# Gated layer: one-hots of the slot places on POOL, spread over a whole unit, with the routed blocks in the five units behind it

## Chip, core and metric

The kernel runs on one core of a Trainium2 chip. The metric is the device time of one execution in microseconds (us). The core has five instruction queues that run beside one another and wait for each other through semaphores: PE (matmul; PEld is its weight load), DVE (vector), ACT (activations), POOL (GpSimd, which here also issues the gathers and scatters) and SP (plain DMAs). Each queue works in its own fixed order.

## The reference, cut to what matters

The program is a stack of four layers on an activation of 4 x 512 x 256 in f32; each layer adds an attention-like part and a feed-forward part. The change touches the routed experts of the third layer (index 2) and of the fourth (index 3). In the third layer, seven small experts serve 2048 tokens, two for each token:

```python
logits = x @ router_w + router_b
probs = jax.nn.sigmoid(logits)
scores, idx = jax.lax.top_k(probs, TOPK)          # TOPK = 2, NR = 7 experts
scores = scores / jnp.sum(scores, axis=-1, keepdims=True)
w = jnp.sum(jax.nn.one_hot(idx, NR, dtype=x.dtype) * scores[..., None], axis=-2)
combined = jnp.zeros_like(x)
for e in range(NR):
    combined = combined + w[..., e:e + 1] * expert_ffn(x, r_gate[e], r_up[e], r_down[e])
```

with `expert_ffn(x, g, u, d) = (silu(x @ g) * (x @ u) / 8) @ d`. Beside it, the same layer computes a gated chunk recurrence with 16 heads (q, k, v, s from projections, two scans, a softmax between them, a norm, a gate and an output projection). The fourth layer has a causal attention and eight experts, again two for each token.

## The kernel before, in words

**The routed experts.** A kernel with fixed shapes cannot loop over "the tokens of expert e". So `dispatch` gives every pair (token, choice) a slot: slots are sorted by expert, each expert's share is filled up to whole blocks of 128 slots, and a block has one expert. For the third layer that makes 38 blocks, for the fourth 39. The steps of `dispatch` are: `rank` and `count` by two matmuls, a chain of small DVE operations that ends in `slot`, `v8` and `slots`, then `whole`, `first` and `inside` (block start and place within the block), and then the inversion of the table: which token sits in slot s? It is done by matmul. For each of 16 tiles of 128 tokens and each of the two choices, `place` is a one-hot of 128 x 128 (which of 128 places), `token` is 128 x 38 (the token's number in the column of its block), and `place` times `token` is added up in the PSUM tile `in_slot`. That makes 32 pairs of one-hots and 32 matmuls (64 passes in the trace, since f32 takes two). Both one-hots have four buffers. When the last matmul is done, `in_slot` is copied out as integers, and `experts_of_blocks` finds each block's expert.

**The blocks.** Each routed block passes through four stages: `fetch2` loads the expert's packed weights `we` by SP (the expert's number is read into a register from `expert`) and gathers the 128 rows `r` by an indirect DMA that POOL issues; `features2` finds share and destination (`mine`, `both`, `share`, `to` on DVE) and transposes the rows (`rt` on PE, `rT` on ACT); `hidden2` does the two projections (`gu`), silu on ACT and the product `h` on DVE; `output2` multiplies by the third weight (`o`, L1160), scales it on ACT (`y`) and scatters it to `l_outs` with another indirect DMA on POOL. `r` has three buffers.

**The gated layer.** Its work is cut into 32 units, a pair of heads times a batch entry. A unit is a generator (`gated_unit`), and two others run with it: `gated_supply` prepares the next unit (projections `pj`, exponentials `eF`, their running sum and reciprocals `rz`, transposes) and `gated_drain` finishes the last one (transposes `ot`, output projection `o`, L1382). Inside the unit, `pov` is the second product with the values; behind it DVE computes `o` and `ms`, and POOL computes `rs` and scales `o` with it (L1355 to L1362).

**The order.** `run(u, beside, rate)` takes the 19 steps of a unit in a written order (L1061) and, after each, adds `rate` to a credit; each whole credit takes one step of a second generator `beside`. The credit starts from zero in each unit. In units 0 to 23 `beside` is the other attention of the layer, in units 24 to 29 it is `routed2`, which is `dispatch` followed by the 38 blocks in their four staggered stages. Unit 30 has `ended2` beside it, which collects `l_outs` (`collect`, L364: loads `sum`, additions on POOL and DVE) and starts the fourth layer's norm; unit 31 has `ahead3`. The order that these generators give is a priority; a scheduler then lays the instructions of each queue in order, so the diff alone does not show where they come to lie.

**The fourth layer.** In `layer3` the PE order is the order of the program. `slots_on()` takes a step of that layer's `dispatch` at high priority; steps of two causal attention units stand between the calls. Behind the first call comes `next(units[1])`, which issues the eight `vp` matmuls.

The functions that the diff touches are these:

Of the kernel before, what the change touches and what calls it, by code (L numbers as in the profile page):

```python
# [9 lines left out]
ALU = mybir.AluOpType  # L10
# [32 lines left out]
class Ring:  # L43
# [19 lines left out]
    def tile(self, shape, dtype, tag, name, bufs=None):  # L63
        if self.alias:
            return self.pool.tile(shape, dtype, tag=self.alias, name=name)
        if tag not in self.places and self.pool is None:
            n = 1
            for d in shape[1:]:
                n *= d
            self.places[tag] = [self.base[:, self.free + i * n : self.free + (i + 1) * n] for i in range(bufs)]  # L70
            self.free += bufs * n
            assert self.free <= self.base.shape[1]
        if tag not in self.places:
            return self.pool.tile(shape, dtype, tag=tag, name=name, **({"bufs": bufs} if bufs else {}))
        i = self.turn.get(tag, 0)
        self.turn[tag] = i + 1
        ap = self.places[tag][i % len(self.places[tag])][: shape[0], :]
        if len(shape) == 3:
            ap = ap.rearrange("p (a b) -> p a b", b=shape[2])
        return ap  # L80


class Net:
# [81 lines left out]
    def dispatch(self, moe, rows, top, w, wk, pool, tag, keep=None):  # L165
# [3 lines left out]
        nc = self.nc  # L169
# [43 lines left out]
        slots = tile("slots", P, NTILE, k)  # L213
# [21 lines left out]
        inside, first, less = tile("inside", P, NTILE, k), tile("first", P, NTILE, k), tile("less", P, NTILE)  # L235
# [7 lines left out]
        for i in range(NTILE):  # L243
            for m in range(k):
                place = wk.tile([P, P], F32, tag="place", name="place", bufs=4)
                nc.vector.tensor_scalar(place, self.lane, inside[:, i, m : m + 1], None, ALU.is_equal)
                token = wk.tile([P, blocks], F32, tag="token", name="token", bufs=4)
                nc.vector.tensor_scalar(
                    token, self.starts[:, :blocks], first[:, i, m : m + 1], less[:, i : i + 1], ALU.is_equal, ALU.mult
                )  # L250
                nc.tensor.matmul(
                    ps, place, token, start=(i == m == 0), stop=(i == NTILE - 1 and m == k - 1)
                )
            if i % 2:
                yield
        moe["in_slot"] = in_slot = tile("in_slot", P, blocks, dt=mybir.dt.uint32, of=keep)
        last = nc.vector.tensor_scalar(in_slot, ps, float(NB * T), None, ALU.add)
        with self.tc.issue_after(last.ins):
# [762 lines left out]
    def layer2(self):  # L1021

        nc, a = self.nc, self.a
        UNITS = 8 * NB

        first, beside = 24, 0.44
        moe = self.moe2
        with ExitStack() as ctx:  # L1030
            tp = lambda n, bufs, **k: ctx.enter_context(self.tc.tile_pool(name=n, bufs=bufs, **k))
            self.gp = gp = {"wk": tp("ga", 1), "wk2": tp("ga2", 2), "ps": tp("gaps", 4, space=PSUM)}
            gp["gn"] = gn = gp["wk"].tile([P, 1], F32, tag="gn", name="gn")
            self.load(gn, a["l2_gn"])
            weights, units = self.weights, {}

            def supplied(u):
                pair, b = u // NB, u % NB
                for _ in norms[b]:
                    pass  # L1040
                if pair not in weights:
                    weights[pair] = self.gated_weights(pair)
                units[u] = {"b": b, "w": weights[pair]}
                return self.gated_supply(units[u])

            def normed(b):
                self.layer_norm(b)
                yield
                self.to_features(
                    gp["ps"], self.xn[:, 4 * b : 4 * b + 4, :], self.xnT[:, :, b * T : (b + 1) * T], tag="ps"  # L1050
                )
                yield

            def run(u, beside, rate):


                supply = supplied(u + 1) if u + 1 < UNITS else iter(())
                drain = self.gated_drain(units[u - 1]) if u else iter(())
                credit = 0.0
                chains = {"m": self.gated_unit(units[u]), "s": supply, "d": drain}  # L1060
                for what in "mmmmsmsmmdmmsmsdmsd" if u + 1 < UNITS else "mmmmdmmdmmdmmm":  # L1061
                    next(chains[what], None)
                    credit += rate
                    while credit >= 1:
                        credit -= 1
                        next(beside, None)

            norms = [normed(b) for b in range(NB)]
            for it in (norms[0], supplied(0)):
                for _ in it:  # L1070
                    pass
            with ExitStack() as lctx:
                lp = self.lp
                lp["wk"] = lctx.enter_context(self.tc.tile_pool(name="la", bufs=1))
                lp["w"] = lctx.enter_context(self.tc.tile_pool(name="laps", bufs=4, space=PSUM))
                latent = self.latent_chain()
                for u in range(first):
                    run(u, latent, beside)
                for _ in latent:
                    pass  # L1080
            wk = tp("ex", 4)
            gp["ex"] = tp("exps", 4, space=PSUM)
            self.router3()
            routed = self.routed2(wk)
            for u in range(first, UNITS - 2):
                run(u, routed, 1.45)
            for _ in routed:
                pass
            run(UNITS - 2, self.ended2(wk, gp["ex"]), 0.75)
            run(UNITS - 1, self.ahead3(gp["ex"]), 1.0)  # L1090
            drain = self.gated_drain(units[UNITS - 1])
            for chain in (self.units3[0], self.units3[0], drain, self.units3[0], drain, drain):
                next(chain, None)
        self.held.close()
# [616 lines left out]
    def layer3(self):  # L1711
        nc, a = self.nc, self.a
        with ExitStack() as ctx:
            tp = lambda n, bufs, **k: ctx.enter_context(self.tc.tile_pool(name=n, bufs=bufs, **k))
            self.wexp = tp("wexp3", 4)
            wp = tp("l3w", 1)
            moe = self.moe3
            self.wk3, we = tp("l3k", 2), tp("l3e", 4)
            self.ps3 = ps3 = {n: tp("l3" + n, bufs, space=PSUM) for n, bufs in (("tr", 2), ("sm", 2), ("mm", 4))}
            psm = ps3["sm"]  # L1720


            with self.tc.manual_schedule(engines={mybir.EngineType.PE}):
                units = self.units3
                route = self.route3(NB - 1, psm, "sm")
                with self.tc.high_priority():
                    self.layer_norm3(NB - 1)
                next(units[0])
                for _ in range(2):
                    with self.tc.high_priority():  # L1730
                        next(route)
                    next(units[1])
                next(units[1])
                pieces = self.wexp.tile([P, 3, 4, D], F32, tag="we", name="pieces")
                pieces = Ring(pieces.rearrange("p q e d -> p (q e d)"), None)
                slots = self.dispatch(moe, self.rows, self.top3, self.w3, pieces, psm, "sm", wp)

                def slots_on():
                    with self.tc.high_priority():
                        return next(slots, slots) is None  # L1740

                slots_on()
                next(units[1])
                for n, _ in enumerate(step for pair in zip(units[0], units[1]) for step in pair):
                    if n >= 4:
                        slots_on()
                while slots_on():
                    pass
                for blocks in self.by_blocks(moe, 1):
                    self.blocks3(blocks, we)  # L1750
            self.collect(moe, Ring(self.rows.rearrange("p i d -> p (i d)"), self.small, {"sum": (8, 2, D)}))
# [289 lines left out]
```

## Time and profile before

| what | value |
|---|---|
| median of three runs | 2280.44 us (2271.02, 2280.44, 2280.53) |
| profiled execution, its own time | 2270.34 us |
| its span, first to last instruction | 2268.5 us |
| mean granted PE clock | 0.914 |
| busy: PE, PEld, DVE, ACT, POOL | 1965.4, 1456.1, 1216.4, 834.0, 614.3 us |
| first and last `in_slot` matmul, third layer | 1585.8, 1604.1 us |
| first gather `r` of the third layer | 1605.03 us |
| first and last `in_slot` matmul, fourth layer | 1947.9, 1979.6 us |

All times within an execution count from the start of the span. A timeline row has start, length, queue, line, operation, output and input, shapes and count (x16 is a group of 16 in a row); the bracket at its end is how long the queue stood idle before it, and what released it. PE rows count passes, and an f32 matmul has two. `PEclk` is the share of the full clock that PE was granted.

### The profile page before, as it was taken

The numbers are of one execution on the slowest core, as the hardware profiler recorded it, in microseconds if no ns is written. First come the engines' busy times: TensorE is split into PE (matmuls) and PEld (weight loads), VectorE is DVE, ScalarE is ACT, GpSimd is POOL, SyncE is SP. The second block draws the span as 40 slices with busy tenths as digits, with TensorE's granted clock in tenths as the row PEclk, the third lists the DMA queues.
The fourth block names the chain that finished last, engine by engine and source line by source line (L and its number), as shares of the span: only waits on it lengthen the run. The fifth ranks groups of instructions, "written<-read, shape, count | busy, mean of one in ns | idle before, by whom it ended". The sixth has DMA issues, their size and how long they took to land.

```text
span 2268.5 us, 35445 instructions
## 1 busy us (share of the span) xinstructions
PE 1965.4 (87%) x13143; PEld 1456.1 (64%) x13143; DVE 1216.4 (54%) x3586; ACT 834.0 (37%) x1693; POOL 614.3 (27%) x727
## 2 busy tenths in 40 slices
PE   6754078867999999999999999999899988899995
PEld 2452067754666676666767676666787776678895
DVE  6765056558565555565565655654565664512323
ACT  1110056543334343343344343434254533334321
POOL 5334734343121211211212111111344342022231
PEclk9955599987999999999999999999799989899998
DMA  9921378773000000000000000000443320157696
GB/s 313 325 69 57 115 239 289 252 250 97 1 13 6 6 12 6 8 15 5 3 15 6 6 13 6 24 13 7 139 126 114 106 84 1 55 210 258 208 329 236
DMA packets 145038, 228.89 MB, mean 101 GB/s; under 512 B 15110, under 2 KB 107624, under 8 KB 144712
## 3 DMA queue, kind: packets, MB, share of 16 engines
q1 hardware_dynamic: 130776, 186.82, 25.6%
q0 software_dynamic: 14064, 39.55, 5.0%
q8 instruction: 110, 1.80, 0.3%
q14 instruction: 88, 0.72, 0.1%
HBM read 177.17 MB, written 64.48 MB: 107 GB/s over the span
## 4 chain that ended last, share of the span: by engine, by line
PE 60%; DVE 9%; issue 7%; POOL 5%; DMA 4%; ACT 2%; SPq 0%; POOLq 0%; DVEq 0%; ACTq 0%
PE pt L1269 8%; PE pj L1191 6%; PE o L1382 4%; PE g L1792 4%; PE kq L1607 3%; PE sc L1254 3%; PE pov L1333 3%; PE gu L988 2%; PE qk L1575 2%; DVE junk L1582 2%; DMA r<-l_rows,in_slot 2%; PE o L1805 2%; PE pv L1623 2%; POOL l_outs L360 1%; PE qkp L1883 1%
## 5 line engine op out<-in xcount | busy, mean ns | idle before, releaser
L360 POOL DMA_INDIRECT l_outs<-y,to x156 | 153.4, 983 | 308.9 <-ACT y L359 218.5
L1582 DVE CUSTOM_DVE_ANT_0 junk<-qk,hide 128x512 f32<-128x512 f32 (+3 forms) x256 | 124.5, 486 | 44.2 <-PE qk L1575 25.3
L1792 PEld LDWEIGHTS g<-rT,we 128*128 128x128 f32 x1120 | 132.3, 194 | 6.4 <-ACT rT L353 4.3
L1792 PE MATMUL g<-rT,we 128*128 128x128 f32 x1120 | 133.1, 278 | 3.1 <-ACT rT L353 3.1
L1615 POOL TENSOR_SCALAR_AFFINE_SELECT pr<-pr 128x512 f32<-128x512 f32 x64 | 40.2, 640 | 344.2 <-ACT pr L1612 344.2
L320 POOL DMA_INDIRECT r<-l_rows,in_slot x73 | 71.1, 974 | 220.8 <-PE rt L351 106.8
L1269 PE MATMUL pt<-Wg,xnT 128*128 128x256 f32 x512 | 127.6, 403 | 2.2 <-ACT h L1154 1.0
L1382 PE MATMUL o<-Wo,oT 128*128 128x256 f32 x512 | 124.2, 385 | 0.0
L1269 PE MATMUL pt<-Wv,xnT 128*128 128x256 f32 x512 | 121.1, 388 | 0.0
L1260 DVE TENSOR_TENSOR s<-sc,keep 128x512 f32<-128x512 f32 x128 | 82.3, 682 | 71.2 <-PE sc L1254 71.2
L1269 PEld LDWEIGHTS pt<-Wg,xnT 128*128 128x128 f32 x512 | 99.8, 201 | 27.6 <-issue 6.3
L1204 DVE RECIPROCAL rz<-rz 128x128 f32<-128x128 f32 x128 | 117.2, 933 | 0.4
L439 PE MATMUL tr<-ident,xn 128*128 128x128 f32 x160 | 36.6, 371 | 92.2 <-DVE xn L424 85.1
L988 PE MATMUL gu<-rT,we 128*128 128x128 f32 x664 | 98.3, 287 | 19.9 <-issue 6.9
L359 ACT ACTIVATE y<-o,share 128x256 f32<-128x256 f32 x156 | 74.0, 474 | 110.1 <-PE o L1805 41.1
L332 DVE TENSOR_TENSOR mine<-r,number 128x2 f32<-128x2 f32 (+2 forms) x90 | 14.8, 164 | 185.0 <-DMA r<-l_rows,in_slot 168.9
L988 PEld LDWEIGHTS gu<-rT,we 128*128 128x128 f32 x664 | 90.9, 198 | 30.9 <-issue 16.0
L1269 PEld LDWEIGHTS pt<-Wv,xnT 128*128 128x128 f32 x512 | 95.4, 192 | 15.2 <-issue 0.2
L1612 ACT ACTIVATE pr<-kq 128x512 f32<-128x512 f32 (+1 forms) x192 | 86.2, 530 | 49.5 <-PE kq L1607 49.0
L1382 PEld LDWEIGHTS o<-Wo,oT 128*128 128x128 f32 x512 | 96.5, 198 | 8.2 <-issue 0.5
L353 ACT COPY rT<-rt 128x256 f32<-128x256 f32 x156 | 57.0, 371 | 117.0 <-PE rt L351 95.8
L1607 PE MATMUL kq<-q,kT 32*128 32x128 f32 (+3 forms) x512 | 89.7, 491 | 7.7 <-DVE mx L1582 5.9
(485 smaller groups left out, 4426.0 us busy)
## 6 DMA issues: line engine op xcount, KB each, us to landing
we<-l_packed SPq DMA_DIRECT2D x121, 384.0 KB
we<-l_w SPq DMA_DIRECT2D x70, 512.0 KB
we<-l_wo SPq DMA_DIRECT2D x35, 512.0 KB
l_rows<-none SPq DMA_DIRECT2D x1, 12920.0 KB
r<-l_rows SPq DMA_DIRECT2D x16, 680.0 KB
xn<-l_outs SPq DMA_DIRECT2D x32, 256.0 KB
l_rows<-xn SPq DMA_DIRECT2D x8, 544.0 KB
l_packed<-l_w_gate SPq DMA_DIRECT2D x1, 4096.0 KB
```

The lines of the kernel that those rows point to most:

```text
L359: nc.scalar.activation(y, ps, AF.Copy, scale=share)
L360: self.no_order(moe["name"] + " back", nc.gpsimd.indirect_dma_start(out=moe["outs"][:, :], out_offset=bass.IndirectOffsetOnAxis(ap=to, axi ...
L988: nc.tensor.matmul(ps[:, q, :], we[:, q, k * P : (k + 1) * P], rT[:, k, :], start=(k == 0), stop=(k == KD - 1))
L1191: nc.tensor.matmul(ps, w[n][:, k, :], self.xnT[:, k, t["b"] * T : (t["b"] + 1) * T], start=(k == 0), stop=(k == KD - 1))
L1204: inverse = lambda c: nc.vector.reciprocal(rz[:, c * P : (c + 1) * P], rz[:, c * P : (c + 1) * P])
L1260: nc.vector.tensor_tensor(s, ps[hh], keep4, ALU.mult)
L1269: nc.tensor.matmul(ps[:, i, :], self.xnT[:, k, s : s + P], w[n][:, k, :], start=(k == 0), stop=(k == KD - 1))
L1382: nc.tensor.matmul(ps[:, p, :], of_parity(oT[:, h, c * D : (c + 1) * D], p), wo[:, h, :], start=(h == 0), stop=(h == 1),)
L1582: nc.vector.tensor_tensor_reduce(out=junk[:, :m], in0=tiles[j][:, off : off + m], in1=self.hide[:, T - m :], op0=ALU.add, op1=ALU.max, sca ...
L1607: nc.tensor.matmul(tiles[j][:, BLOCK[i] - off : BLOCK[i] - off + T - i * P], kT[r, i * P : (i + 1) * P], qT[r, i * P :], start=True, stop= ...
L1612: nc.scalar.activation(pr[:, j, off : off + m], tiles[j][:, :m], AF.Exp, scale=0.25)
L1792: nc.tensor.matmul(pt[:, m, :], we[:, q, k * T + m * P : k * T + (m + 1) * P], rT[:, k, :], start=(k == 0), stop=(k == KD - 1),)
```

## The change

There are three edits. In `dispatch`, `place` is made by POOL (`nc.gpsimd`) where the experts are those of the third layer, and by DVE elsewhere; and the loop over the 16 tiles yields after each tile, where it yielded after every second. In `layer2`, the first of the six units takes 0.95 steps of `routed2` for each of its own and the other five take 1.62, where all took 1.45. In `layer3`, `slots_on` takes two steps of `dispatch` at each call where it took one, at its first call too.

```diff
@@ dispatch
         for i in range(NTILE):
             for m in range(k):
                 place = wk.tile([P, P], F32, tag="place", name="place", bufs=4)
-                nc.vector.tensor_scalar(place, self.lane, inside[:, i, m : m + 1], None, ALU.is_equal)
+                (nc.gpsimd if moe is self.moe2 else nc.vector).tensor_scalar(place, self.lane, inside[:, i, m : m + 1], None, ALU.is_equal)
                 token = wk.tile([P, blocks], F32, tag="token", name="token", bufs=4)
...
-            if i % 2:
-                yield
+            yield
         moe["in_slot"] = in_slot = tile("in_slot", P, blocks, dt=mybir.dt.uint32, of=keep)
@@ layer2
             for u in range(first, UNITS - 2):
-                run(u, routed, 1.45)
+                run(u, routed, 0.95 if u == first else 1.62)
             for _ in routed:
                 pass
@@ layer3
                 def slots_on():
                     with self.tc.high_priority():
-                        return next(slots, slots) is None
+                        return next(slots, slots) is None and next(slots, slots) is None
```

## The prediction

> **What bounds the kernel now.** I read the page's shares and slices first, then the PE timeline around the routed work of the gated layer, the stretches with their granted clock, the DVE and POOL timelines of the same stretch, the groups by shape for POOL's prices, and last the PE timeline at the start of layer 3, because the diff touches `slots_on` there.
>
> ```profile
> PE 1965.4 (87%) x13143; PEld 1456.1 (64%) x13143; DVE 1216.4 (54%) x3586; ACT 834.0 (37%) x1693; POOL 614.3 (27%) x727
> PEclk9955599987999999999999999999799989899998
> ```
>
> PE is the bound: 87% busy. In the clock row, slice 28 (1588 to 1645 us) shows 7 where the gated layer otherwise has 9. That is where the one-hots of the slot places lie.
>
> ```profile
> core 0: us, PE busy (x) PEld busy (x) DVE busy (x) ACT busy (x) POOL busy (x), PEclk, DMA share, GB/s
> 1585.00:1588.00 3.00, 2.90 (x23) 2.37 (x24) 2.97 (x16) 0.00 (x0) 0.00 (x0) 0.94 0.37 123
> 1588.00:1609.00 21.00, 19.81 (x86) 18.97 (x86) 15.90 (x67) 0.59 (x1) 3.00 (x3) 0.50 0.32 103
> 1609.00:1612.00 3.00, 3.00 (x22) 2.55 (x21) 1.70 (x12) 0.87 (x3) 0.73 (x1) 0.57 0.98 319
> ```
>
> From 1588 to 1609 us PE is nominally full, but at clock 0.50, and POOL is nearly idle. The `in_slot` matmuls (38 columns) keep PE occupied without keeping its clock up.
>
> ```profile
> 1594.64 9.87 PE L251 MATMUL in_slot<-token,place 128*128 128x38 f32 x46
> 1605.70 3.33 PE L1333 MATMUL pov<-v,s 128*128 128x128 f32 x14 [1.19 <-DVE of L276]
> 1617.05 0.70 PE L1160 MATMUL o<-we,h 128*128 128x256 f32 x2 [1.65 <-DVE h L1155]
> 1628.99 1.22 PE L1160 MATMUL o<-we,h 128*128 128x256 f32 x2 [4.47 <-DVE h L1155]
> 1840.65 1.12 PE L1302 MATMUL okt<-ident,ok 128*128 128x128 f32 x4 [4.41 <-DVE ok L1298]
> 1848.65 1.09 PE L1375 MATMUL ot<-ident,o 128*128 128x128 f32 x4 [2.64 <-ACT oT L1376]
> ```
>
> The bracket is PE's idle time before the group. Three costs can be seen: 23 in_slots in a row at 0.43 us each, then 1.19 us until `pov`; 1.65 + 4.47 us while the pipeline of routed blocks fills; and 4.41 + 2.64 us in unit 30, where `collect` puts its additions in front of `ok` on DVE.
>
> ```profile
> 1597.72 0.29 DVE L246 TENSOR_SCALAR place<-lane,inside 128x128 f32<-128x128 f32 x1
> 1597.92 0.30 DVE L248 TENSOR_SCALAR token<-starts,first,less 128x38 f32<-128x38 f32 x1
> 1605.03 1.09 POOL L320 DMA_INDIRECT r<-l_rows,in_slot  x1 [32.34 <-DVE past L275]
> ```
>
> One pair takes DVE 0.42 us start to start, so DVE too paces the run of in_slots. POOL waits 32 us for the end of it.
>
> **The change part by part.** The built queue orders of both kernels show what moves. No instruction of the work is added: 32 `place` go from DVE to POOL and everything else is reordered. The dispatch has 1 + 16 yields instead of 1 + 8, and the blocks 38 x 4 = 152. A unit has 19 steps: before, six units took floor(27.55) = 27 each; after, unit 24 takes 18 and five units floor(30.78) = 30 each. So the first block moves from unit 24 into unit 25, and the density rises from 27/4 = 6.75 to 7.5 blocks a unit. PE's own work stays the same, so that alone costs nothing; POOL, with 7.5 pairs of gather and scatter at 2.6 us and 4.1 us of `rs` work per 40 us unit, stays below 60%.
>
> *A, the slot places in unit 24.* They cannot start before `inside` (1585.0), so they cover half of unit 24: 22 in_slots stand before `pov`, 8 between the `pov` and `turn` matmuls, 2 among the first scores of unit 25. POOL has all 32 `place` in one row, before the `rs` of that unit. The trace shows no such operation on POOL; the nearest rows:
>
> ```profile
> L1359 POOL TENSOR_TENSOR rs<-rs,neghalf 128x8 f32<-128x8 f32 x32 | 52.7, 1648 | 2.5
> L1362 POOL TENSOR_TENSOR o<-o,rs 128x512 f32<-128x512 f32 x64 | 65.4, 1042 | 2.5
> L580 POOL TENSOR_SCALAR sg<-sg 128x512 f32<-128x512 f32 x8 | 12.1, 1515 | 17.5 <-ACT sg L579 17.5
> L403 POOL TENSOR_SCALAR rs<-mv 128x4 f32<-128x4 f32 x16 | 4.1, 255 | 33.9 <-DVE mv L414 32.6 <-DVE xn L212 1.1
> ```
>
> The same operation costs 192 ns at 4 columns undisturbed (a row of L403's other tile) and 1515 at 512, so 128 columns are 0.19 + 124 x 2.6 ns = 0.52 us. [...] I take the row, 0.52. [...]
>
> ```profile
> L1839 DVE TENSOR_SCALAR xn<-x,mv,rs x16: 401/406/1362, 1842.6 to 1921.9; 128x256 f32<-128x256 f32 x16
> ```
>
> The 1362 ns are one instance that met an addition on POOL. If each `token` on DVE excludes each `place`, a pair takes 0.52 + 0.21 = 0.73 us, and place 32 ends at 1585.3 + 23.4 = 1608.7 instead of 1602. [...] PE needs for the same stretch, at half clock, 8 `sc` 1.9 + 4 `turn` 1.0 + 4 `o` 3.4 + 22 x 0.43 = 15.8 us, less 1.2 for the first warm 2.7 us: until 1599.6. [...] From there to the end of `pov`, at half clock: 6 x 0.43 + 3.3 + 1.6 = 7.5, so 1607 against 1611.4 before; 4 in_slots are then outstanding (1.5) and one `rt` (0.4) is not yet done. A gains 1611.4 - 1607 - 1.9 = 2.5 us. Ends: 9 gained if the clock stays full (then PE is fed by POOL alone), 0 if the exclusion is complete. I take 2.5, because in_slots with 38 columns held the clock at 0.50 before too.
>
> DVE is relieved of 32 x 0.20 = 6.4 us, but behind `token` (4 buffers) it now waits for POOL's pace: the second and third `rz` reciprocals, the `s` of `pov`, and `o`, `ms` of unit 24 are queued there. `s` stands behind token 22, which needs in_slot 18: 4 in_slots of slack (1.7 us) against 1.3 us for both `s`. Just hidden; if POOL were slower it would come straight onto PE.
>
> *B, the pipeline's start in unit 25.* On POOL the first five gathers now stand behind `rs` (0.25 + 1.67 + 2.04 us), which waits for `ms` 2.9 us after the end of `pov` (P). They start at P + 7.3 and land 2.9 us later (gather 1605.03, first use 1607.94), at P + 10.2. PE reaches the first `rt` at P + 8.1 at full clock, P + 10 at half: 0 to 2 us of wait. Then `h` of block 0 on DVE stands behind `mine` of block 3, whose gather needs the buffer of block 0: about 2 us more. On SP the first nine `we` loads fall behind a `Wo` load; the `expert` register comes at P + 6.4 and `Wo` is free by then, so this costs nothing. Against 1.65 + 4.47 us of idle and 1.6 us of half clock behind it before, B gains 7.7 - 4.2 = 3.5 us. Ends: 7 gained, 2 lost (`rs` as the new gate).
>
> *C, unit 30.* The last `o` of the blocks moves behind four scores of unit 30, and two scatters instead of one stand behind `rs` on POOL: `collect` starts 1.3 us later. `ok` moves up in front of two bn_stats (0.8 us earlier), and on ACT `oT` now stands before the copies scaled by `again`, so the 2.64 us wait should go; but four sums instead of three stand before the layer norm's `rs` on POOL (+1.4 us). DVE is full from 1851 on and gives most of it back. I take 1.5 gained; ends 5 gained, 3 lost.
>
> *D, layer 3.* `slots_on` now runs two steps at its first call. The two in_slots of tile 0 stand directly behind `count` on PE, ahead of the eight `vp` matmuls that covered the DVE chain until now.
>
> ```profile
> 1933.12 0.39 PE L180 MATMUL count<-mt,ones 128*128 128x128 f32 x2
> 1933.34 3.62 PE L1894 MATMUL vp<-both,yT 128*128 128x256 f32 x16
> 1942.11 0.33 PE L1905 MATMUL pt<-ident,s 128*128 128x128 f32 x1 [3.39 <-ACT s L1925]
> 1939.85 0.48 DVE L246 TENSOR_SCALAR pieces<-lane,pieces 128x128 f32<-128x128 f32 x2
> ```
>
> The first `place` ends on DVE near 1940.4; PE stands idle for 7.1 us from 1933.4. Then come 2 in_slots, `vp` and the scores with the first 3.5 us at half clock, and the softmax chain of the first scores (2.5 us): first `pt` at 1949.3 instead of 1942.1, +7.2. The scores behind it, at half clock before (5.9 us), run warm (4.3): -1.6. At the end 2 in_slots fewer stand before `o`: -0.6. D loses 5 us; ends 3.5 and 8. Nothing else can hide it: the next idle times of PE (1.00, 1.00, 2.02) wait for DVE and ACT work that moves along.
>
> Sum: -2.5 - 3.5 - 1.5 + 5 = -2.5 us. The profiled execution took 2270.3 (span 2268.5), so 2267.8. The four executions shown lie in two groups, 2270.3 and 2271.0, 2280.4 and 2280.5; the median is of the upper one, so the forecast on its scale is 2280.4 - 2.5 = 2278. 0.5% is 11.4 us, about what a measurement of this kernel tells from no change.
>
> **The rivals.** *R1, the clock stays up.* The in_slots between real matmuls leave the PE clock at 1.00, and the pipeline starts without a gap: -9 - 7 - 5 + 4 = -17, so 2263. For it: the in_slots stand among real matmuls, where before 23 of them stood alone from 1594 on. Against it: the clock fell at 1588 already, while scores and `o` were still mixed in.
>
> *R2, POOL becomes the gate (slower).* A `place` costs 1.2 us or more, by a slow compare or by exclusion. Place 22 then comes at 1585.3 + 26.4 = 1611.7 instead of about 1600, and `pov`, `rs` and the gathers slip by the same 12 us: -2.5 + 12 + 4 (no gain left in B) = +14, so 2294. It decides from about 0.85 us on, where place 22 comes at 1604 and A is gone. For it: L580's steep 2.6 ns a column; against it: L403's 192 ns and L1362's 1042 ns at 512 columns.
>
> *R3, the change hardly does what it says.* The slot places spread over half a unit, PE stays at half clock and is fed no faster: A is 0, sum 0, 2280.4.
>
> **How the numbers follow.** Forecast 0.60 (of which 0.07 reach past +11 us, with D at its far end and B lost), R1 0.17, R2 0.13, R3 0.10. Faster by over 0.5%: 0.17. Within: 0.53 + 0.10 = 0.63. Slower: 0.13 + 0.07 = 0.20. The range 2258 to 2290 takes in the lower group of executions with a gain of 12, and the upper one with a loss of 10.
>
> **What would show it.** A: the clock between 1588 and 1609, `place` on POOL at 0.5 us, `pov` ending near 1607. B: `rt` of block 0 waiting 0 to 2 us, one `o` waiting near 2. C: no wait of `ot` for `oT` in unit 30. D: an idle time of about 7 us before `in_slot` behind `count`. The forecast is wrong if `place` takes over 0.85 us, if PE's clock stays full in unit 24, or if D does not show.

## The result, and the profile after

The changed kernel is slower: 2290.57 us median against 2278.58 us of the kernel before in the same runs, a ratio of 1.0073 with a 95% interval of 1.005 to 1.0095. That is 16.6 us (11 to 22). The forecast was 2278, a gain of 2.5 us, with a range up to 2290.

The profiled execution took 2291.72 us with a span of 2289.9; that of before had 2268.5. Of these 21.4 us, 4.2 were there before any changed instruction ran: the first `sc<-q,eF` of unit 24 starts at 1584.97 before and at 1589.16 after, with the same work ahead of it. So every comparison below counts from a matmul that both kernels have. The page of the kernel after, its busy times and its clock row:

```profile
PE 1982.7 (87%) x13143; PEld 1465.7 (64%) x13143; DVE 1213.3 (53%) x3558; ACT 836.1 (37%) x1691; POOL 634.3 (28%) x759
PEclk9955599988999999999999999998899988899998
```

PE has the same 13143 instructions and 17 us more busy time, so part of the loss lies in matmuls that took longer, at a lower clock (0.909 granted in the mean, 0.914 before). The line numbers of the kernel after are one lower behind L254.

**Unit 24, the slot places.** The stretches of the kernel after, with the clock's fall and rise as borders (columns: length, then busy time and count of PE, PEld, DVE, ACT, POOL, then granted clock, DMA share, GB/s):

```profile
1589.20:1591.90 2.70, 2.22 (x17) 1.69 (x17) 2.10 (x10) 0.00 (x0) 2.48 (x4) 0.99 0.26 90
1591.90:1619.20 27.30, 27.30 (x110) 24.34 (x109) 14.75 (x37) 2.37 (x4) 17.79 (x31) 0.50 0.22 74
1619.20:1622.20 3.00, 3.00 (x25) 2.37 (x23) 0.95 (x3) 0.00 (x0) 2.92 (x3) 1.00 0.21 71
```

The half clock lasts 27.3 us; before it was 23.9. POOL's group of the same stretch (busy us, mean ns, idle before):

```profile
L246 POOL TENSOR_SCALAR place<-lane,inside 128x128 f32<-128x128 f32 x32 | 19.4, 620 | 20.6 <-DVE inside L240 12.5 <-PE in_slot L251 8.1
```

A `place` takes 620 ns on POOL in the mean, and POOL waited 8.1 us for buffers that PE had to free. PE waited for a `place` only once, 0.48 us for the first one; from the 23rd on, each `place` was ready 2.4 to 5.7 us before PE loaded it. So it is not POOL's pace that keeps the in_slots apart here, but the fixed order in which the scheduler laid PE's queue: before, 23 of them stand in a row, here never more than four. In the PE timeline:

```profile
1604.85 1.34 PE L251 MATMUL in_slot<-token,place 128*128 128x38 f32 x6
1605.99 2.05 PE L1332 MATMUL pov<-v,s 128*128 128x128 f32 x8
1607.84 0.49 PE L251 MATMUL in_slot<-token,place 128*128 128x38 f32 x2
1608.12 0.78 PE L1332 MATMUL pov<-v,s 128*128 128x128 f32 x2
...
1614.29 0.65 PE L251 MATMUL in_slot<-token,place 128*128 128x38 f32 x2
1614.86 0.79 PE L1338 MATMUL pov<-ev,q 64*128 64x128 f32 x2
1615.59 0.65 PE L251 MATMUL in_slot<-token,place 128*128 128x38 f32 x2
```

`pov` starts 3.9 us earlier after the first scores than before, as planned, but with single in_slots strewn through it at half clock it ends at 1615.65: 26.5 us behind the first scores, where it was 26.4 before. The gain of unit 24 is nothing, and five in_slots (the last row's is the first of them) are still to come.

**Units 26 to 29, the denser blocks.** One row for each unit, before and then after:

```profile
1667.63:1707.14 39.51, 38.52 (x279) 31.56 (x279) 22.02 (x70) 18.02 (x38) 17.92 (x20) 1.00 0.42 126
1707.14:1746.32 39.18, 38.09 (x273) 30.34 (x272) 23.67 (x76) 17.72 (x38) 17.23 (x18) 1.00 0.37 111
1746.32:1785.88 39.56, 38.22 (x279) 31.21 (x278) 23.05 (x75) 20.58 (x41) 16.80 (x17) 1.00 0.38 116
1785.88:1825.28 39.40, 38.90 (x282) 31.76 (x281) 22.12 (x60) 20.17 (x40) 14.59 (x17) 1.00 0.27 79
```

```profile
1665.36:1707.87 42.51, 40.12 (x291) 32.52 (x290) 23.06 (x76) 18.64 (x41) 19.04 (x20) 1.00 0.42 132
1707.87:1749.22 41.35, 39.18 (x284) 32.08 (x283) 24.47 (x82) 20.82 (x42) 18.44 (x19) 1.00 0.39 117
1749.22:1792.33 43.11, 40.13 (x292) 32.54 (x291) 23.33 (x76) 18.62 (x41) 19.04 (x20) 1.00 0.38 121
1792.33:1834.78 42.45, 40.30 (x292) 33.03 (x291) 22.95 (x70) 21.29 (x43) 17.20 (x18) 1.00 0.31 89
```

The clock is full in both. Length minus busy PE is idle time: 3.9 us in the four units before, 9.7 after. These 5.8 us stand in no line of the prediction. Who PE waits for, in the groups of the same four units (busy us, mean ns, idle before and its releasers), before and after:

```profile
L1160 PE MATMUL o<-we,h 128*128 128x256 f32 x56 | 18.0, 404 | 2.1 <-DVE h L1155 1.8 <-issue 0.3
```

```profile
L1159 PE MATMUL o<-we,h 128*128 128x256 f32 x61 | 19.6, 401 | 8.1 <-DVE h L1154 8.0
```

It is `o`, the third matmul of a block, that waits for `h`. One of these waits in the timelines of PE and DVE after:

```profile
1716.41 0.70 PE L1159 MATMUL o<-we,h 128*128 128x256 f32 x2 [1.67 <-DVE h L1154]
```

```profile
1715.14 0.16 DVE L331 TENSOR_TENSOR mine<-r,number 128x2 f32<-128x2 f32 x1 [3.53 <-DMA r<-l_rows,in_slot]
1715.34 0.16 DVE L336 TENSOR_TENSOR both<-mine,r 128x2 f32<-128x2 f32 x1
1715.42 0.15 DVE L337 TENSOR_TENSOR both<-mine,layers 128x2 f32<-128x2 f32 x1
1715.61 0.16 DVE L339 TENSOR_REDUCE share<-both 128x2 f32<-128x4 f32 x1
1715.80 0.16 DVE L340 TENSOR_TENSOR share<-share,r 128x1 f32<-128x1 f32 x1
1715.99 0.16 DVE L342 TENSOR_TENSOR to<-share,beyond 128x1 uint32<-128x1 f32 x1
1716.07 0.28 DVE L1154 SCALAR_TENSOR_TENSOR h<-gu,h 128x128 f32<-128x128 f32 x1
```

DVE stands 3.53 us at `mine` of a later block, whose gathered rows have not landed. `h`, whose inputs have been there since 1712.60 (the end of ACT's silu), is queued behind it, and `o` behind `h`. The wait of DVE costs nothing by itself; it costs because something that PE needs stands behind it.

**Unit 30 and the fourth layer**, PE timeline after:

```profile
1849.98 0.66 PE L1301 MATMUL okt<-ident,ok 128*128 128x128 f32 x4 [3.29 <-DVE ok L1297]
1853.04 1.09 PE L1374 MATMUL ot<-ident,o 128*128 128x128 f32 x4 [0.53 <-DVE eF L1200]
1948.63 0.39 PE L180 MATMUL count<-mt,ones 128*128 128x128 f32 x2
1956.82 1.04 PE L251 MATMUL in_slot<-pieces 128*128 128x39 f32 x4 [7.80 <-DVE pieces L246]
1957.66 5.10 PE L1893 MATMUL vp<-both,yT 128*128 128x256 f32 x16
```

In unit 30 the two waits shrink from 4.41 and 2.64 to 3.29 and 0.53 us, but a new wait of 2.28 us, of `pvt` for ACT, takes their place, and the stretch from `okt` to the next first `sc<-q,eF` is 18.86 us instead of 18.67. In the fourth layer PE idles 7.80 us between `count` and the first in_slot, and `vp`, which ran in that time before, comes behind it at a granted clock of 0.72 (5.10 us), where before it had 1.00 (3.62 us).

### The profile page after: what moved, and what is told of

It is laid out like the page before. It is cut to its first block, busy times and chain, and to the rows that moved or that the text cites. A ratio compares the mean times of both kernels' runs of the same rounds, so it can differ in the third digit from the quotient of the medians.

```text
span 2289.9 us, 35481 instructions
## 1 busy us (share of the span) xinstructions
PE 1982.7 (87%) x13143; PEld 1465.7 (64%) x13143; DVE 1213.3 (53%) x3558; ACT 836.1 (37%) x1691; POOL 634.3 (28%) x759
## 4 chain that ended last, share of the span: by engine, by line
PE 58%; issue 9%; DVE 8%; POOL 5%; DMA 4%; ACT 2%; SPq 0%; POOLq 0%; DVEq 0%; ACTq 0%
PE pt L1268 8%; PE pj L1190 6%; PE o L1381 4%; PE kq L1606 3%; PE pov L1332 3%; PE sc L1253 3%; PE gu L987 3%; DMA r<-l_rows,in_slot 2%; PE qk L1574 2%; POOL l_outs L359 2%; DVE junk L1581 2%; PE pv L1622 2%; PE g L1791 1%; PE st L1241 1%; PE o L1000 1%
## 5 line engine op out<-in xcount | busy, mean ns | idle before, releaser
L438 PEld LDWEIGHTS tr<-ident,xn 128*128 128x128 f32 x160 | 25.1, 186 | 102.6 <-issue 59.1
```

## The experiments

Differences are the ratio's, times the median of the kernel before in the same runs. "First part" means the changed kernel with the fourth layer of before. The ranges in brackets are 95% intervals of the ratio; 0.001 of it is 2.3 us. Where a number is the difference of two experiments, it has the uncertainty of both.

**1. One step at the first `slots_on`: the fourth layer as before.**

```diff
-                slots_on()
+                with self.tc.high_priority():
+                    next(slots)
                 next(units[1])
```

> The changed kernel, but the first slots_on of the fourth layer takes one step as before, so that the fourth layer is that of the kernel before. In the traces the changed kernel lost 17.5 us from the first scores of unit 24 to the end (the two executions stood 4.2 us apart already): about 6 in units 24 to 29, 4 in unit 31 under a half clock, 8 in the fourth layer. Theory (several causes, each its own): the 8 us of the fourth layer go, 2279 + 10 = 2289 at most, 2285 if unit 31's half clock was chance; vp directly behind count, no idle time between. Rival (what the fourth layer loses is carried in from the third): no difference to the changed kernel, about 2291 to 2295.

Measured: 1.0046 (1.003 to 1.0061), +10.4 us, 6 less than the whole change. `vp` stands directly behind `count` again. In its trace unit 24 has 27.3 us of half clock and units 26 to 29 have 8.7 us of idle PE, like the changed kernel. The third and the fourth layer each have a loss of their own.

**2. Only the fourth layer's part.**

```diff
-            if i % 2:
+            if i % 2 or moe is self.moe3:
                 yield
...
-                        return next(slots, slots) is None
+                        return next(slots, slots) is None and next(slots, slots) is None
```

> The kernel before with only the fourth layer's part of the change: one tile of slot places a step there, two steps at each slots_on, the first too; the third layer is that of the kernel before. Theory: +8 us (7 us of idle PE in front of the first in_slot, and half clock behind it): 2287. The prediction's middle value: +5, 2284. Rival (in_slots ahead of vp cost nothing, all is lost in the third layer): 2279.

Measured: 1.0036 (1.002 to 1.0052), +8.1 us. With experiment 1 that makes 18.5, against 16.6 for the whole: the two add up within their intervals. The PE timeline has the wait:

```profile
1918.80 1.04 PE L251 MATMUL in_slot<-pieces 128*128 128x39 f32 x4 [7.81 <-DVE pieces L246]
```

From the start of the projections `qkp` to the first `pt` it takes 24.1 us instead of 16.2, and at the first block's `g` 8.6 us of delay are still there: nothing behind the wait gives it back.

**3. The same, but the first `slots_on` behind `vp`.**

```diff
-                slots_on()
                 next(units[1])
+                slots_on()
```

> As the kernel with only the fourth layer's part of the change (+8.2 us measured), but the first slots_on stands behind the step that issues the eight vp matmuls instead of ahead of it. Theory (the loss is that PE waits for the DVE chain with nothing queued ahead of the first in_slots): no idle time of 7 us any more, 0 to +1 against before. Rival (the finer steps of one tile cost in themselves, by more switches and half clock): +5 to +8.

Measured: 1.0043 (1.0024 to 1.0062), +9.8 us. By its numbers the theory fell, but I had overlooked what moves: the first step of `slots_on` holds `rank` and `count` as well, so these went behind `vp` too, and the DVE chain that they feed started about 3.5 us later, behind all eight of them:

```profile
1945.46 0.39 PE L180 MATMUL count<-mt,ones 128*128 128x128 f32 x2
1953.67 1.04 PE L251 MATMUL in_slot<-pieces 128*128 128x39 f32 x4 [7.82 <-DVE pieces L246]
```

The idle time is again 7.8 us, because again nothing stands between `count` and the in_slots. What counts is not whether `vp` is ahead of the in_slots, but whether it lies between them and `count`. In experiment 1 it does, and there the wait is gone.

**4. The first part with `place` on DVE: spreading and density alone.**

```diff
-                (nc.gpsimd if moe is self.moe2 else nc.vector).tensor_scalar(place, ...
+                nc.vector.tensor_scalar(place, ...
```

> As the first of these (the changed kernel with the fourth layer of before), but place is made by DVE, so that only the spreading and the densities of units 24 to 29 are left of the change. Theory (the density of blocks and the half clock cost, the engine of place does not): within 2 us of the run with place on POOL, about 2285 to 2289. Rival (POOL is the gate: 0.60 us for place where 0.43 us for an in_slot is the pace of PE): 3 to 5 us faster than with place on POOL.

Measured: 1.0022 (1.0003 to 1.004), +5.0 us, 5.4 less than with `place` on POOL. The rival's number came in, though the intervals of the two (0.7 to 9.0 us and 6.8 to 13.8) overlap. Its reason did not: with the engine of `place` PE's order moved too. In this trace 13 in_slots stand in a row ahead of `pov`, where with POOL never more than four do. The stretch of unit 24 has 17.1 us of half clock instead of 27.3 and is 6.0 us shorter. The order of this run with `place` on POOL was not run, so engine and order are not separated by a run; that each late `place` was ready long before its turn speaks for the order.

**5. Only `place` on POOL, the rest of the program as before.**

```diff
-                nc.vector.tensor_scalar(place, self.lane, ...
+                (nc.gpsimd if moe is self.moe2 else nc.vector).tensor_scalar(place, self.lane, ...
```

> The kernel before with place on POOL and nothing else changed. Here 23 in_slots stand in a row without other PE work. Theory: place at 0.60 us each instead of DVE's pair at 0.42 us sets the pace of these 23: +0.18 x 23 = +4 us up to pov, and the same for the rest of the pipeline: 2283. Rival (PE at half clock sets the pace at 0.43 us, POOL works ahead by four buffers; or a lighter DVE gains): 2279 or less.

Measured: 1.0004 (0.9988 to 1.002), +0.9 us. POOL's `place` took 613 ns here. PE's order moved in this run as well: 13 in_slots in a row are left of the 23 that the expectation counted on. The last of these did run at POOL's pace, 0.59 us each instead of 0.43, but `pov` started only 1.3 us later, not 4. So POOL's price alone isn't the loss; it needs the spread order.

**6. Only the two rates.**

```diff
-                run(u, routed, 1.45)
+                run(u, routed, 0.95 if u == first else 1.62)
```

> The kernel before with only the rates of the change: 0.95 in unit 24, 1.62 behind it. Slot places on DVE in pairs of tiles as before (they need 9 of the 18 steps that unit 24 now takes), blocks at 7.5 to 8 a unit from unit 25 on. Theory (the density alone makes o wait for h): idle time of PE in units 26 to 28 at 2 us or more each (0.9 to 1.3 before), +3 to +6 us in all. Rival (only the spread slot places cost, the density nothing): idle time as before, 0.

Measured: 1.0017 (1.0004 to 1.0031), +3.8 us. The `o` group of units 26 to 29:

```profile
L1160 PE MATMUL o<-we,h 128*128 128x256 f32 x59 | 18.8, 398 | 7.2 <-DVE h L1155 7.2
```

The rates alone bring 7.2 us of waits for `h` instead of 1.8. All traces agree: idle PE in front of this `o` is 1.8 to 2.4 us in the eight with the old rates, and 6.6 to 8.1 in the seven that have the new ones without the round of stages of experiment 8. The later start of the blocks, which these rates bring too, shortened the idle PE of unit 25 to 3.0 us (6.6 before), so the +3.8 us hold that gain already.

**7. A fourth buffer for `r`, in the first part and in the kernel before.**

```diff
-        r = wk.tile([P, n, EXT], F32, tag="r", name="r", bufs=3)
+        r = wk.tile([P, n, EXT], F32, tag="r", name="r", bufs=4 if moe is self.moe2 else 3)
```

> The changed kernel with the fourth layer of before, and in the third layer a fourth buffer for the gathered rows r, so that a gather is issued one block earlier. Three executions with the denser blocks show 8 to 9.4 us of idle PE in four units (3.6 in the kernel before), nearly all in front of an o that waits for h, which stands on DVE behind a mine that waits for its gather. Theory (late gathers cause these waits): the idle time of units 26 to 29 falls to 4 us or less, and the time by about 5 us against the same kernel with three buffers (which was +10.4 us against before): +5. Rival (the steps follow each other too closely for ACT and DVE, whatever the gather does): idle time stays at 8 or more, +10.

> The kernel before with a fourth buffer for the gathered rows r in the third layer, nothing else. Theory: with 6.75 blocks a unit the gathers are hardly late; of 3.6 us of idle time in units 26 to 29 about 1.8 wait for h, and some of the 4 to 6 us while the pipeline fills: -2 to -4 us. Rival (three buffers were enough at this density): 0.

Measured: 1.0064 (1.0044 to 1.0083), +14.6 us, for the first part, and 1.0022 (1.001 to 1.0035), +5.0 us, for the kernel before. Neither gained. In the first part `o` waited 7.7 us for `h` (6.9 without). The gathers were issued no earlier; this one waits for an `rt` as its like did in the changed kernel (4.16 us there):

```profile
1706.19 0.98 POOL L319 DMA_INDIRECT r<-l_rows,in_slot  x1 [4.17 <-PE rt L350]
```

So the buffer was not what set the gather's time, and the run says nothing on late gathers. Why the kernel before became 5 us slower with it stays open: its trace shows no new wait of that size in the third layer.

**8. One round of stages between a gather and its use** (first part, `place` on DVE; a fifth buffer for `we`, three for `place`).

```diff
-        stages = self.fetch2, self.features2, self.hidden2, self.output2
+        stages = self.fetch2, lambda t, wk, *state: state, self.features2, self.hidden2, self.output2
...
-                    yield
+                    if s != 1:
+                        yield
```

> The changed kernel with place on DVE and the fourth layer of before (+5.0 us measured), and the features stage of a block one round of stages later than its gather (a fifth buffer for we, a third instead of a fourth for place, to fit), densities as in the changed kernel. Theory (at this density the time from issuing a gather to mine is shorter than the gather, and h stands behind mine): the waits of mine on DVE fall from 46 us to under 10, those of o for h in units 26 to 29 from 7 to 2 us, 0 to +1 us against before. Rival (h is late for another reason, ACT or the reciprocals on DVE): the waits of o stay at 6 us or more, +5.

Measured: 1.0007 (0.9991 to 1.0023), +1.6 us, 3.4 less than experiment 4 at the same density, with intervals that overlap (-2.0 to 5.2 us and 0.7 to 9.0); the clearer pair stands in experiment 10. Its `o` group:

```profile
L1160 PE MATMUL o<-we,h 128*128 128x256 f32 x62 | 20.2, 407 | 2.8 <-DVE h L1155 2.8
```

The waits for `h` fall from 6.6 to 2.8 us, which supports the theory. Its other number missed: `mine` still waits 44 us in sum on DVE, and an `h` still stands directly behind waits of up to 4.9 us. But PE comes to the `o` of that `h` later, and does not wait. The two changes of buffers were not run alone at this density.

**9. Three copies of `token` side by side: more columns for each in_slot**, in the kernel before and in the first part.

```diff
-                token = wk.tile([P, blocks], F32, ...
+                token = wk.tile([P, 3, blocks], F32, ...
...
-                    token, self.starts[:, :blocks], first[...
+                    token, self.starts[:, :blocks].unsqueeze(1).to_broadcast([P, 3, blocks]), first[...
```

> The kernel before, with token of the third layer written three times side by side (114 columns instead of 38), so that each in_slot matmul moves three times the columns through the same weights. Theory (the short moving operand lets the PE clock fall): the half clock in unit 24 (24, 17 and 24 us in three executions of this instruction order) falls below 8 us, and the time changes by -6 to 0 although the matmuls are longer. Rival (the clock falls for another reason): half clock as before or longer, each in_slot longer by 76 columns in two passes, about 0.1 us at full clock and 0.2 at half: +3 to +7 us.

> The changed kernel with the fourth layer of before (+10.4 us), and token of the third layer written three times side by side (114 columns instead of 38). [...] Theory (the spread in_slots pull every window below the bar): half clock in unit 24 under 14 us instead of 27, +4 to +8 us against before. Rival (half clock comes from waiting, not from columns): 27 us or more at half clock, and +13 or more.

Measured: 1.0005 (0.9992 to 1.0018), +1.2 us, in the kernel before: half clock in unit 24 fell only to 17.1 us, so neither side's numbers came in. In the first part 1.0037 (1.0017 to 1.0057), +8.4 us, and 13.7 us of half clock in unit 24 instead of 27.3, as expected. PE's order moved here too (up to six in_slots in a row ahead of `pov` instead of four), so that the columns alone did it is not shown. The bar that the theory speaks of was an estimate of mine, and no run shows one. With 114 columns the in_slots took PE 15.6 us in the kernel before, where they had taken 14.0, and 14.2 us in the first part (15.6 in the changed kernel). The intervals of +8.4 and +10.4 overlap, so a gain in time is not shown either.

**10. Places alternately on POOL and DVE**, in the kernel before, in the first part, and in experiment 8.

```diff
-                nc.vector.tensor_scalar(place, ...
+                (nc.gpsimd if moe is self.moe2 and m else nc.vector).tensor_scalar(place, ...
```

> The kernel before with every second place of the third layer on POOL (0.60 us) and the others on DVE, in the old order. DVE's pace for a pair falls from 0.42 to about 0.32 us, POOL's is 0.30 a pair. Theory (PE is fed by DVE there): the 23 in_slots in a row take 7.5 instead of 9.9 us, -2 us. Rival (at half clock an in_slot takes PE 0.43 us anyway): 0.

> The changed kernel with the fourth layer of before (+10.4 us), with only every second place on POOL and the others on DVE: POOL then makes a place in 0.60 us for every two in_slots. Theory (POOL's pace strings the in_slots out until behind pov, at half clock): as with all on DVE or better, +3 to +5 us against before, half clock in unit 24 at 10 to 17 us instead of 27. Rival (the spread order itself keeps the clock down): half clock stays at 27 us, +9 to +11.

> As the run with one stage more between gather and features (spread slot places, dense blocks, fourth layer of before; +1.6 us), but place alternately on POOL and DVE. Theory (all named losses taken away): -2 to +1 us against before. Rival (what remains is the fill of the pipeline and half clock that no order here removes): +1 to +3.

Measured, kernel before: 1.0004 (0.9984 to 1.0023), +0.9 us. PE's run of in_slots did speed up, but no time came of it:

```profile
1579.48 6.45 PE L251 MATMUL in_slot<-token,place 128*128 128x38 f32 x40
```

At full clock (until 1584.6) a pair takes 0.31 us in its steady part. In experiment 2, whose run of 23 stood at full clock for its first 4.3 us, it took 0.40 to 0.41, so DVE had been feeding PE there. At half clock, as in the kernel before, PE's own 0.43 us set the pace. The idle PE of unit 25, where the pipeline fills, was then 8.0 us, but it was 6.6 before and 4.3 in experiment 2 with one and the same order, so single traces don't tell whether the fill took the gain.

First part: 1.0019 (0.9999 to 1.0038), +4.3 us, where POOL alone had +10.4. Half clock in unit 24 of its trace was 3.4 us. The three versions of the spread, over unit 24 from the first `sc<-q,eF` to the first `sc<-qT,kT`: on POOL (experiment 1), on DVE (experiment 4), and on both, here and in the run with experiment 8, whose order of PE is the same in this stretch:

```profile
1568.42:1599.39 30.97, 30.54 (x128) 26.67 (x129) 16.80 (x47) 2.37 (x4) 21.17 (x34) 0.56 0.22 73
```

```profile
1574.72:1599.68 24.96, 24.75 (x125) 22.22 (x125) 18.90 (x72) 2.36 (x4) 0.09 (x1) 0.66 0.27 91
```

```profile
1585.57:1605.66 20.09, 19.16 (x124) 16.59 (x124) 15.61 (x56) 2.15 (x4) 9.68 (x15) 0.92 0.34 113
```

```profile
1579.47:1604.69 25.22, 24.92 (x124) 22.17 (x124) 15.57 (x56) 2.15 (x4) 9.62 (x15) 0.66 0.27 90
```

Nearly the same work (30 in_slots in the first, 28 in the others) takes 31, 25, and 20 or 25 us, at clocks of 0.56, 0.66, and 0.92 or 0.66. So the 20 us were in part luck: the same order gave 25 in another execution. What repeats is the order with all places on POOL: 27.3 us of half clock in all three traces that have it (the changed kernel and experiments 1 and 7), against 3.4 to 17.1 in the four traces of the other two versions.

Experiment 8 with places on both: 0.9984 (0.9968 to 1.0000), -3.6 us. In the same runs that is 7.9 us less than without the round of stages, and the two intervals (-7.3 to 0 and -0.2 to 8.6) hardly touch. It is the only version that came out below the kernel before, and its interval ends at no difference. It keeps the change's spreading and density, and undoes the three things that cost: the first call in the fourth layer, all places on POOL, and the short way from a gather to its use.

**11. One round of stages more in the kernel before.** The edit of experiment 8 in the old order and density.

> The kernel before with the features stage one round of stages later than its gather, as in the run with one stage more, and a fifth buffer for we, a third instead of a fourth for place; order and densities as before. Theory (at 6.75 blocks a unit little waits): 1.8 us of waits of o for h go, the fill of the pipeline grows by as much: -2 to +2. Rival (the waits of the fill, 4 to 7 us, are made by late gathers and shrink): -3 to -5.

Measured: 1.0012 (0.9996 to 1.0027), +2.7 us. At 6.75 blocks a unit there was little to win, and it was not won.

## Why the prediction was wrong, by its own steps

- **The step that failed first** is the sentence that the rise from 6.75 to 7.5 blocks a unit "alone costs nothing", because PE's work stays the same. I had looked only at how full POOL would be. The two rates cost +3.8 us (experiment 6), although they hold B's gain, and a round of stages more takes 7.9 back in experiment 10. The waits of `mine` for gathers were in the trace of before, as idle DVE, and `o` waited 1.8 us for `h` there; I didn't ask what would stand behind those waits at a closer pace.
- **A, the slot places, -2.5 us.** Wrong in sign, and by size the step that failed most. Of the first part's +10.4 us, 3.8 are those of the rates; the other 6.6 are A and C, and C is about 0. With `place` on DVE instead, 1.2 are left (5.0 - 3.8), which is no more than the noise of two experiments. The price of `place` was nearly right: 0.62 us where I took 0.52. `token` and `place` didn't exclude each other: 30 of 32 `token` ran beside a `place`, and took 304 ns in the median where they had taken 299. What failed is the end of A's sum: the in_slots were set there at the half-clock price of before, 0.43 us each, with PE at the 22nd by 1599.6 and `pov` ending at 1607. Counted from the same first scores, `pov` started at 1601.8 and ended at 1611.5, five in_slots were outstanding instead of four, and the half clock lasted 27.3 us. I took the half clock as given by the in_slots' columns; with the same 38 columns it lasted 23.9 us in the order of before, 27.3 in that of the changed kernel, and 17.1 with `place` on DVE (experiment 4).
- **B, the pipeline's start, -3.5 us.** Right in kind. The idle PE of unit 25 fell from 6.6 us to 3.3, and a single wait of 2.78 us for `h` is left where I expected about 2, but 3.4 us of half clock follow it as before. The size stays open: in experiments 2, 3 and 7 (its second run), with the order of before, that idle time was 4.3 to 5.8 us.
- **C, unit 30, -1.5 us.** The wait of `ot` for `oT` did go, and the one for `ok` shrank, but `pvt` then waited 2.28 us, and the stretch is no shorter. About 0.
- **D, layer 3, +5 us.** The idle time was named with its place and size (7.1 predicted, 7.8 found). The first `pt` came 8.0 us later in experiment 2, where I had 7.2. The two refunds behind it failed: the stretch from there to `ov` was 0.4 us shorter instead of 1.6, and that to the first `o` 0.5 us longer instead of 0.6 shorter. So D is +8.1, just past the far end of my 3.5 to 8.
- **The rivals.** R1 fell: the clock stayed down longer instead of up, and that is what the trace of before had said against it. R3 is not it either. R2 had the right engine and nearly the right time (2294), but by luck: its way there, 12 us of delay of `pov` at 1.2 us a `place`, did not occur, and the time is near because the rates and D cost too. A `place` took 0.62 us, below its bar of 0.85, and POOL never kept PE waiting for long: 0.5 us of idle PE up to `pov`. The loss goes through PE's order and clock, not through a wait.

Together: +6.6 (A and C), +3.8 (the rates, with B in them) and +8.1 (D) make +18.5, against 16.6 (11 to 22) measured. That unit 31 in the two first traces differs by 4.3 us is no part of it: it had 0 us of half clock in one and 10.2 in the other, and in the other traces, with either order, between 0 and 13.7.

## What to carry to other kernels

When an interleaving is made denser, look at the in-order queues of the side engines for instructions that wait for a transfer, and ask what PE needs from behind them; a round of stages between issue and use removed most of that here (6.6 us of waits for `h` became 2.8), a further buffer did not (6.9 became 7.7). Before an instruction is moved ahead on PE, find the producer chain it waits for and check that independent work still lies between the head of that chain and the instruction. Look also at the clock of real work that cheap matmuls are strewn through: here both stood at half clock for 27.3 us, in all three traces of that order. And when a producer is moved to another engine, look at the order that the scheduler then lays for the consumer: here that order moved, while PE hardly waited for the new producer (0.5 us).

## What the runs showed of the hardware

In the traces of before and after the granted PE clock was 1.00 or 0.50 at any time. The stretches of half clock in unit 24 lasted 3.41, 10.24, 13.65, 17.07, 23.89 and 27.31 us in the traces of this study. Busy time did not tell the clock: PE counts as busy for all 27.30 us of half clock after the change, and for 22.71 of the 23.90 us before.

In unit 24 the half clock lasted 23.9 us with 23 in_slots in a row (before), 27.3 us with the in_slots spread and `place` on POOL (after), and 17.1 us with 13 in a row and `place` on DVE (experiment 4). What in PE's work brought the clock down, and what brought it up again, is not shown. Experiment 9, where the same matmuls had 114 columns instead of 38 and the half clock of the first part was 13.7 us instead of 27.3, moved the order as well.

One and the same order did not always have the same half clock. Six traces have the same order of PE in the stretch of unit 24 (the kernel before and experiments 2, 3, 6, 11 and the second of 7): five had 23.9 us of half clock there and took 29.9 us, and that of experiment 2 had 10.2 and took 25.1. What made this difference is not shown. It is more than most effects of this study. A single profile could not have told them apart; the repeated runs did.
